# A factorised interaction network: one transfer per shifted tile from a DRAM copy of x, products of 2048 columns in a hand-written order, and weights prepared by another route

## The chip, the core and the metric

The kernel runs on one core of a Trainium2 chip. The metric is the device time of one execution in microseconds. The engines are TensorE (PE, matmuls into PSUM; PEld are its weight loads), VectorE (DVE), ScalarE (ACT), GpSimd (POOL) and SyncE (SP). SP, ACT and POOL can issue transfers (DMA) between DRAM and SBUF, the on-chip memory of 128 partitions.

## What is computed

The input x has 1024 samples of 39 fields of 64 embedding values. Three layers take products of fields:

```python
def _cin_layer(Xk, X0, W, b):
    O = W.shape[0]
    Hk, Fdim = (Xk.shape[1], X0.shape[1])
    Wr = W.reshape(O, Hk, Fdim)
    return jnp.einsum('bhe,bfe,ohf->boe', Xk, X0, Wr) + b[None, :, None]
X0 = sparse_embedding
Xk = X0
outs = []
for W, b in ((W0, b0), (W1, b1), (W2, b2)):
    Xk = _cin_layer(Xk, X0, W, b)
    outs.append(Xk.sum(axis=-1))
cin_output = jnp.concatenate(outs, axis=-1)
return cin_output @ fc_w.T + fc_b
```

Everything is float32. Each layer has 64 outputs; the result is one number per sample.

## The kernel before

**The algebra.** A column is one (sample, embedding) pair: 65536 columns of 39 values. The second and third layer reach the output only through fc_w, so the weights are contracted first, on the chip: V1 and V2 are 64 x 39 tables made from W1, W2 and fc_w, and T (64 x 39 x 39) is W1 contracted with V2. Then y is a sum over columns of X1 (Z + fc0) + c x, where X1 and Z are two 64-row results of one matrix product over the 780 unordered pairs of fields of a column.

**Pairs by shifted tiles.** A tile r_i (i = 0 to 3) has 117 partitions, three groups of 39 rows; each group holds x with its fields rolled by some shift. The elementwise product of two such tiles holds 117 pairs per column. Six products of two tiles and a seventh, of r_0 with a tile q of [x shifted by 17; x; ones], give all pairs, the squares and x itself. So a column costs seven products on VectorE and seven accumulated matmul chunks on PE, whose weights `wt` hold [T | W0] rows gathered to match the pairs.

**Blocks.** The loop over n takes 32 blocks of 2048 columns (`BLK`). SP issues all of a block's transfers, in this order: the load of 39 rows of x into the first group of r_0 (L175, runs of 64 values), two copies of these rows into r_0's other groups (L178, L179), nine copies with a shift into r_1 to r_3 (L183), and two into q (L184, L185). Each is 39 rows of 8 KB, 312 KB, from SBUF to SBUF but for the load. The copies wait for the load, and shifted copies read rows that earlier copies wrote. The r tiles have two buffers each, so a block's transfers can run while the block before is computed.

**The inner loop.** Each block has two halves of 1024 columns (`SUB`). For each half VectorE makes seven products p (L193, ten buffers), and PE takes each in two matmuls of 512 columns into a PSUM tile po (L195; the profile counts a float32 matmul as two instructions, 56 per block). When a half is done, ACT adds the bias to X1 (L204) and copies x's rows into g (L206), VectorE forms (Z + fc0) X1 (L207) and sums over the 64 embedding values (L209). The order on each engine is chosen by the framework's scheduler. At the very end two matmuls with a column of ones and c (L216) and ACT (L217) give y.

**Weights.** ACT issues the loads of w1 and w2, then fc. V2 comes from eight matmuls of one output row (L103), each copied by VectorE (L105) and spread by a transfer of its own (L106); V1 the same way in five (L114 to L117). T comes from five matmuls (L122), copied into `table` beside W0 (L123). The table is written four times, doubled both ways, to DRAM (`wide`, L131), and 39 gathers on ACT (L137) read it into wa and wb by strided rows, so that a roll needs no wrap. `wt` is wa + wb (L148): one addition that waits for all gathers.

**Semaphores.** Transfers issued by SP and ACT signal their landing on eight semaphores (DMAHW0 to DMAHW7 in the rows below), used again and again by both queues; a transfer that takes a semaphore waits until the one before it on that semaphore has landed. POOL's transfers have eight of their own (DMASW).

Of the kernel before, what the change touches and what calls it, by code (L numbers as in the profile page):

```python
# [24 lines left out]
[x shifted by LAST; x; 1], gives that one, the squares and x itself.  # L25
"""
# [16 lines left out]
SHIFT = ((0, 1, 3, 10), (0, 4, 15, 20), (0, 6, 14, 27))  # L43
LAST = 17
# [6 lines left out]
SB = SUB // E  # L51

_dist = sorted(
    min((s[k] - s[i]) % F, (s[i] - s[k]) % F) for s in SHIFT for i, k in PAIRS
)
assert sorted(_dist + [LAST]) == list(range(1, F // 2 + 1))


@with_exitstack
def cin_kernel(ctx: ExitStack, tc: tile.TileContext, x, w0t, b0, w1, b1, w2, b2, fc_w, fc_b, out):  # L60
    nc = tc.nc
    PSUM = bass.MemoryType.PSUM

    const = ctx.enter_context(tc.tile_pool(name="const", bufs=1))
    prep = ctx.enter_context(tc.tile_pool(name="prep", bufs=2))
    dram = ctx.enter_context(tc.tile_pool(name="dram", bufs=1, space=bass.MemoryType.DRAM))
# [3 lines left out]
    ps_prep = ctx.enter_context(tc.tile_pool(name="ps_prep", bufs=2, space=PSUM))  # L70
    ps_main = ctx.enter_context(tc.tile_pool(name="ps_main", bufs=3, space=PSUM))

# [1 line left out]
    w1s = const.tile([H, FH], F32, name="w1s")  # L74
    nc.scalar.dma_start(w1s, w1)
    w2s = const.tile([H, FH], F32, name="w2s")
    nc.scalar.dma_start(w2s, w2)
    fc = const.tile([H, 3], F32, name="fc")
    nc.scalar.dma_start(fc, fc_w.rearrange("o (l h) -> h (o l)", h=H))
# [8 lines left out]
    # table[b, a] = [T[:, a, b] | W0[:, a, b]]  # L88
    table = const.tile([F, F, 2 * H], F32, name="table")
    nc.scalar.dma_start(table[:, :, H:], w0t)  # L90
# [3 lines left out]
    wt = const.tile([K, NCHUNK, 2 * H], F32, name="wt")  # L94
    nc.vector.memset(wa[:, NCHUNK - 1, :], 0.0)
    nc.vector.memset(wb[:, NCHUNK - 1, :], 0.0)

# [1 line left out]
    v2 = const.tile([H, F], F32, name="v2")  # L99
    for g in range(8):  # L100
        n = 8 * F
        pv = ps_prep.tile([128, MM], F32, name="pv", tag="pp")
        nc.tensor.matmul(pv[0:1, :n], fc[:, 2:3], w2s[:, g * n : (g + 1) * n], start=True, stop=True)  # L103
        vrow = prep.tile([1, MM], F32, name="vrow", tag="vrow")
        nc.vector.tensor_copy(vrow[:, :n], pv[0:1, :n])  # L105
        nc.scalar.dma_start(v2[8 * g : 8 * g + 8, :], vrow[:, :n])  # L106

# [1 line left out]
    w1v = w1s.rearrange("o (h f) -> o f h", f=F)  # L109
    for g in range(5):  # L110
        f0, f1 = 8 * g, min(8 * g + 8, F)
        n = (f1 - f0) * H
        pv = ps_prep.tile([128, MM], F32, name="pv", tag="pp")
        nc.tensor.matmul(pv[0:1, :n], fc[:, 1:2], w1v[:, f0:f1, :], start=True, stop=True)  # L114
        vrow = prep.tile([1, MM], F32, name="vrow", tag="vrow")
        nc.vector.tensor_copy(vrow[:, :n], pv[0:1, :n])  # L116
        nc.scalar.dma_start(wa[2 * F + f0 : 2 * F + f1, NCHUNK - 1, 0:H], vrow[:, :n])  # L117
    for g in range(5):
        f0, f1 = 8 * g, min(8 * g + 8, F)
        n = (f1 - f0) * H  # L120
        pt = ps_prep.tile([128, MM], F32, name="pt", tag="pp")
        nc.tensor.matmul(pt[0:F, :n], v2, w1v[:, f0:f1, :], start=True, stop=True)  # L122
        nc.vector.tensor_copy(  # L123
            table[:, f0:f1, 0:H], pt[0:F, :n].rearrange("p (f h) -> p f h", h=H)
        )

# [1 line left out]
    wide = dram.tile([2 * F, 2 * F, 2 * H], F32, name="wide")  # L128
    for i in range(2):
        for k in range(2):  # L130
            nc.scalar.dma_start(wide[i * F : (i + 1) * F, k * F : (k + 1) * F, :], table)  # L131
    pair_rows = wide.rearrange("b a h -> (b a) h")

    def gather(dst, c, j, sa, sb):
        first = sb * 2 * F + sa
        step = 2 * F + 1
        nc.scalar.dma_start(  # L137
            dst[j * F : (j + 1) * F, c, :], pair_rows[first : first + (F - 1) * step + 1 : step, :]
        )

    for c, (i, k) in enumerate(PAIRS):
        for j in range(NG):
            gather(wa, c, j, SHIFT[j][i], SHIFT[j][k])
            gather(wb, c, j, SHIFT[j][k], SHIFT[j][i])
    gather(wa, NCHUNK - 1, 0, 0, LAST)
    gather(wb, NCHUNK - 1, 0, LAST, 0)
    gather(wa, NCHUNK - 1, 1, 0, 0)
    nc.vector.tensor_tensor(wt, wa, wb, ALU.add)  # L148

# [1 line left out]
    wfin = const.tile([H + F, 1], F32, name="wfin")  # L151
    nc.vector.memset(wfin[0:H], 1.0)
    pc = ps_prep.tile([128, MM], F32, name="pc", tag="pp")
    nc.tensor.matmul(pc[0:F, 0:1], v2, bias[:, 0:1], start=True, stop=True)  # L154
# [9 lines left out]
    for i in range(2):  # L164
        qt = const.tile([K, BLK], F32, name=f"q{i}")
        nc.gpsimd.memset(qt, 1.0)  # L166
        q.append(qt)
# [93 lines left out]
```

## Time and profile before

| | |
|---|---|
| median of 3 runs | 1157.2 us (1156.73 to 1162.63) |
| the profiled execution, first to last instruction | 1157.6 us |
| PE busy | 887.4 us, 77% |
| DVE busy | 682.9 us, 59% |
| ACT busy | 140.9 us, 12% |
| POOL busy | 3.7 us |
| mean granted clock of PE | 0.915 |
| moved by DMA | 149.09 MB, mean 129 GB/s |

The profile comes from one execution. Its page gives each engine's busy time; the chain that ended last (followed back from the last instruction, at each step to whatever released it); groups of instructions by line with total and mean duration and what ended the idle time before them; and transfers by queue. Other views list instructions in order of time, or give per stretch of time each engine's busy time, the granted clock, the busy share of the 16 DMA engines and the GB/s moved. In the chain "SPq L183" is time in which SP's queue was busy issuing that line's transfers, and "DMA r<-in_x" is time from an issue to the landing. A transfer landed when the engine waiting for it goes on.

### The profile page before, as it was taken

To read this page: it belongs to the slowest core of one execution; us is meant where nothing else is said; L and a number is where in the kernel's file an instruction comes from. 1 tells how busy PE (TensorE), PEld (TensorE's weight loads), DVE (VectorE), ACT (ScalarE), POOL (GpSimd) and SP (SyncE) were. 2 spreads that over 40 slices of the span, in tenths; PEclk is the share of its full clock that TensorE was granted. 3 is DMA by queue.
4 is the path that set the end of the run, shared out by engine and by line. 5 is a ranking of instruction groups with operands and counts; after the bars stand their busy time and mean duration, and the time that the engine had idled before them with its cause. 6 is when DMAs were issued, how large, how long until landed. Compare 5 with 4: busy or idle time off the path is not lost.

```text
span 1157.6 us, 5508 instructions
## 1 busy us (share of the span) xinstructions
PE 887.4 (77%) x1838; PEld 364.8 (32%) x1838; DVE 682.9 (59%) x598; ACT 140.9 (12%) x133; POOL 3.7 (0%) x6
## 2 busy tenths in 40 slices
PE   2700798988887878898787887987778788788887
PEld 0000343333333333333333333332333333333333
DVE  0330567667766656667655566575556666766555
ACT  1000012111111111101111111011111111111111
POOL 1000000000000000000000000000000000000000
PEclk9999999999888888998888889988988998888889
DMA  8463256556556565556566655555665555656650
GB/s 134 110 141 92 60 135 146 133 130 136 136 131 135 135 149 134 127 131 141 130 138 135 140 129 134 130 136 128 140 148 134 127 136 132 142 132 141 142 138 6
DMA packets 66601, 149.09 MB, mean 129 GB/s; under 512 B 48543, under 2 KB 50064, under 8 KB 50065
## 3 DMA queue, kind: packets, MB, share of 16 engines
q1 hardware_dynamic: 61986, 143.16, 54.6%
q10 hardware_dynamic: 4586, 5.59, 2.4%
q8 instruction: 14, 0.23, 0.1%
q14 instruction: 15, 0.11, 0.0%
HBM read 12.67 MB, written 3.12 MB: 14 GB/s over the span
## 4 chain that ended last, share of the span: by engine, by line
SPq 49%; DMA 37%; PE 9%; ACTq 2%; issue 2%; DVE 1%; ACT 0%; DVEq 0%
SPq L183 41%; DMA r<-in_x 17%; DMA r<-r 14%; PE po L195 7%; SPq L185 4%; SPq L184 3%; ACTq L137 2%; DMA v<-vrow 1%; DMA wide<-table 1%; DMA fc<-in_fc_w 1%; PE pt L122 1%; DMA q<-r 1%; DVE p L193 0%; DMA wa<-wide 0%; DMA wa<-vrow 0%
## 5 line engine op out<-in xcount | busy, mean ns | idle before, releaser
L195 PE MATMUL po<-p,wt 117*128 117x512 f32 x1792 | 855.9, 639 | 231.6 <-DVE p L193 149.9
L195 PEld LDWEIGHTS po<-p,wt 117*128 117x128 f32 x1792 | 360.9, 205 | 726.2 <-issue 418.0
L193 DVE TENSOR_TENSOR p<-r,r 117x1024 f32<-117x1024 f32 x384 | 451.1, 1217 | 135.6 <-DMA r<-r 123.5
L207 DVE SCALAR_TENSOR_TENSOR g<-po,fc,x 64x1024 f32<-64x1024 f32 x64 | 81.6, 1276 | 228.0 <-ACT x L204 228.0
L204 ACT ACTIVATE x<-po,b0s 64x1024 f32<-64x1024 f32 x64 | 71.1, 1110 | 760.4 <-PE po L195 760.4
L206 ACT COPY g<-r 39x1024 f32<-39x1024 f32 x64 | 66.8, 1044 | 199.2 <-DVE sums L209 196.3
L193 DVE TENSOR_TENSOR p<-r,q 117x1024 f32<-117x1024 f32 x64 | 77.8, 1216 | 5.4 <-DMA q<-r 4.6
L209 DVE TENSOR_REDUCE sums<-g 103x16 f32<-103x1024 f32 x64 | 77.6, 1212 | 1.1
L148 DVE TENSOR_TENSOR wt<-wa,wb 117x896 f32<-117x896 f32 x1 | 1.1, 1093 | 54.8 <-DMA wa<-wide 54.8
L103 PE MATMUL pv<-w2s,fc 64*1 64x312 f32 x16 | 8.9, 709 | 23.0 <-DMA fc<-in_fc_w 17.2
L105 DVE COPY vrow<-pv 1x312 f32<-1x312 f32 x8 | 3.6, 468 | 29.8 <-PE pv L103 17.9
L114 PE MATMUL pv<-w1s,fc 64*1 64x512 f32 (+1 forms) x10 | 9.7, 1093 | 4.0 <-DVE vrow L105 2.3
L103 PEld LDWEIGHTS pv<-w2s,fc 64*1 64x1 f32 x16 | 1.2, 94 | 29.6 <-DMA w2s<-in_w 17.2
L122 PE MATMUL pt<-w1s,v 64*39 64x512 f32 (+1 forms) x10 | 9.6, 1104 | 0.8 <-DVE table L123 0.8
L216 PE MATMUL py<-sums,wfin 103*1 103x512 f32 x4 | 3.2, 880 | 7.7 <-DVE sums L209 7.7
L123 DVE COPY table<-pt 39x512 f32<-39x512 f32 (+1 forms) x5 | 3.3, 670 | 7.3 <-PE pt L122 7.3
L116 DVE COPY vrow<-pv 1x512 f32<-1x512 f32 (+1 forms) x5 | 3.2, 662 | 7.1 <-DMA wa<-vrow 3.7
L114 PEld LDWEIGHTS pv<-w1s,fc 64*1 64x1 f32 x10 | 0.6, 87 | 12.4 <-DVE vrow L116 6.5
L122 PEld LDWEIGHTS pt<-w1s,v 64*39 64x39 f32 x10 | 1.4, 157 | 9.0 <-DVE table L123 4.2
L206 ACT ACT_TABLE_LOAD x1 | 1.3, 1283 | 21.8 <-DMA v<-vrow 21.8
L155 ACT COPY wfin<-pc 39x1 f32<-39x1 f32 x1 | 0.2, 151 | 28.0 <-PE pc L154 28.0
L166 POOL MEMSET q<- 117x2048 f32 x2 | 3.5, 1804 | 0.3 <-POOLq L248 0.3
(16 smaller groups left out, 3.7 us busy)
## 6 DMA issues: line engine op xcount, KB each, us to landing
r<-r SPq DMA_DIRECT2D x352, 312.0 KB
q<-r SPq DMA_DIRECT2D x64, 312.0 KB
r<-in_x SPq DMA_DIRECT2D x32, 312.0 KB
wide<-table ACTq DMA_DIRECT2D x4, 760.5 KB
w1s<-in_w ACTq DMA_DIRECT2D x1, 624.0 KB
w2s<-in_w ACTq DMA_DIRECT2D x1, 624.0 KB
wa<-wide ACTq DMA_DIRECT2D x20, 19.5 KB
table<-in_w0t ACTq DMA_DIRECT2D x1, 380.2 KB
```

The costliest lines, as they stand in the source:

```text
L114: nc.tensor.matmul(pv[0:1, :n], fc[:, 1:2], w1v[:, f0:f1, :], start=True, stop=True)
L122: nc.tensor.matmul(pt[0:F, :n], v2, w1v[:, f0:f1, :], start=True, stop=True)
L137: nc.scalar.dma_start(dst[j * F : (j + 1) * F, c, :], pair_rows[first : first + (F - 1) * step + 1 : step, :])
L183: nc.sync.dma_start(r[i][j * F : (j + 1) * F], r[0][s : s + F])
L184: nc.sync.dma_start(qt[0:F], r[0][LAST : LAST + F])
L185: nc.sync.dma_start(qt[F : 2 * F], r[0][0:F])
L193: nc.vector.tensor_tensor(p, a[:, cols], b[:, cols], ALU.mult)
L195: nc.tensor.matmul(po[:, bass.ts(m, MM)], wt[:, c, :], p[:, bass.ts(m, MM)], start=(c == 0), stop=(c == NCHUNK - 1),)
L204: nc.scalar.activation(x1, po[H:128, :], AF.Identity, bias=b0s[H:128])
L206: nc.scalar.copy(g[H : H + F], r[0][0:F, cols])
L207: nc.vector.scalar_tensor_tensor(g[0:H], po[0:H, :], fc[:, 0:1], x1, ALU.add, ALU.mult)
L209: nc.vector.tensor_reduce(sums[:, b_at : b_at + SB], g.rearrange("p (b e) -> p b e", e=E), AX.X, ALU.add)
```

## The change

- **A copy of x in DRAM.** `load(n)` brings a block's 39 rows to a staging tile xs; `store(n)` writes them twice, one under the other, to a tile xd of 78 rows in DRAM; `roll(n)` reads each r_i from there in one transfer of 117 rows of 8 KB (936 KB), with rows of the three groups interleaved: partition 3f + j holds x[f + BASE[i] + j STEP[i]]. The shifts form such steps now (STEP, BASE; LAST is 11). q takes its two sets of rows from xd too. A block has 9 transfers instead of 14.
- **Order by hand.** The framework's scheduler is off (`manual_schedule`); each engine takes its instructions as they are written. SP: roll(n + 1), load(n + 2), store(n + 2). VectorE: a product covers 2048 columns (`BLK`, four buffers); the last block's results (`finish`) stand behind this block's fourth product. PSUM is one pool of four two-bank tiles.
- **x's rows for g** are copied from xs, not from r_0.
- **Weights.** fc is the first transfer on ACT, w2 the first on SP. W0 goes from DRAM to a doubled table in DRAM on POOL (`wide0`), and its 15 gathers are POOL's. V2 comes from eight matmuls of 32 equal output rows each, put under each other in PSUM, two copies and two transfers. V2 doubled, with fc1 as two more columns, is the left operand of the five matmuls for T, so that V1 comes out as a row of the same product; each of the five parts is copied and stored twice to DRAM (`wide`, L194) at once. Gathers of T go out on ACT (into wa, L201) and SP (into wb). Each chunk's wa + wb is its own addition (L284), behind that chunk's product of block 0, and the matmuls take wa.

```diff
+STEP = (0, 15, 9, 6)
+BASE = (0, 3, 5, 20)
+LAST = 11
...
+def rows(t, first, steps, n):
+    base = t[:]
+    width = base.ap[-1][1] if len(base.ap) == 2 else n
+    ap = [[s * width, k] for s, k in steps] + [[1, n]]
+    return bass.AP(base.tensor, base.offset + first * width, ap)
...
-    prods = ctx.enter_context(tc.tile_pool(name="prods", bufs=10))
+    prods = ctx.enter_context(tc.tile_pool(name="prods", bufs=4))
...
+    ctx.enter_context(tc.manual_schedule())
...
+    def load(n):
+        xs[n] = stage.tile([F, BLK], F32, name="xs", tag="xs")
+        nc.sync.dma_start(
+            xs[n].rearrange("p (b e) -> p b e", e=E), xv[:, n * BB : (n + 1) * BB, :]
+        )
+    def store(n):
+        xd[n] = xds.tile([FW, BLK], F32, name="xd", tag="xd")
+        nc.sync.dma_start(xd[n][0:F], xs[n])
+        nc.sync.dma_start(xd[n][F:FW], xs[n])
+    def roll(n):
+        r[n] = [rolls.tile([K, BLK], F32, name=f"r{i}", tag=f"r{i}") for i in range(4)]
+        for i in range(4):
+            nc.sync.dma_start(r[n][i], rows(xd[n], BASE[i], [(1, F), (STEP[i], NG)], BLK))
+        qt = q[n % 2]
+        nc.sync.dma_start(qt[0:K:NG], xd[n][LAST : LAST + F])
+        nc.sync.dma_start(qt[1:K:NG], xd[n][0:F])
...
+    for half in range(2):
+        for t in range(4):
+            g = 4 * half + t
+            nc.tensor.matmul(pv[32 * t : 32 * t + 32, half, 0:n8], fc2,
+                w2s[:, g * n8 : (g + 1) * n8], start=True, stop=True)
+    for half in range(2):
+        nc.vector.tensor_copy(vrow[:, half], pv[:, half, 0:n8])
+        nc.scalar.dma_start(v2[32 * half : 32 * half + 32, 0:F], vrow[0:128:32, half])
+    nc.vector.tensor_copy(v2[:, F:FW], v2[:, 0:F])
...
+        nc.tensor.matmul(pt[0:FX, :n], v2, w1v[:, f0:f1, :], start=True, stop=True)
+        part = const.tile([FX, MM], F32, name=f"part{g}")
+        nc.vector.tensor_copy(part[:, :n], pt[0:FX, :n])
+        for k in range(2):
+            nc.scalar.dma_start(widev[:, (k * F + f0) * H : (k * F + f1) * H], part[:, :n])
...
+    for c, (i, k) in enumerate(PAIRS):
+        gather(nc.scalar, wa[:, c], wide, i, k, tcol)
+        gather(nc.sync, wb[:, c], wide, k, i, tcol)
...
+    store(1)
...
-                p = prods.tile([K, SUB], F32, name="p")
-                nc.vector.tensor_tensor(p, a[:, cols], b[:, cols], ALU.mult)
+        p = prods.tile([K, BLK], F32, name="p", tag="p")
+        nc.vector.tensor_tensor(p, a, b, ALU.mult)
...
+            nc.scalar.copy(gt[H : H + F], xs[n][:, bass.ts(h, SUB)])
...
+    for n in range(NBLK):
+        if n + 1 < NBLK:
+            roll(n + 1)
+        if n + 2 < NBLK:
+            load(n + 2)
+            store(n + 2)
+        for c in range(NCHUNK):
+            p = product(n, c)
+            if n == 0:
+                nc.vector.tensor_tensor(wa[:, c], wa[:, c], wb[:, c], ALU.add)
+            multiply(n, c, p)
+            if n > 0 and c == 3:
+                finish(n - 1)
+        fields(n)
+    finish(NBLK - 1)
```

The order on SP in the steady loop, before: one block but for its load and its second q transfer (r_415 is that block's r_0; r_416 to r_418 are r_1 to r_3; in brackets what an instruction waits for).

```order
L178 DMA r_415<-r_415 39x2048 [waits DMAHW5_49,DMAHW4_49]
L179 DMA r_415<-r_415 39x2048 [waits DMAHW6_49]
L183 DMA r_416<-r_415 39x2048 [waits DMAHW7_49,DMAHW5_49]
L183 DMA r_416<-r_415 39x2048 [waits DMAHW0_49]
L183 DMA r_416<-r_415 39x2048 [waits DMAHW1_49]
L183 DMA r_417<-r_415 39x2048 [waits DMAHW2_49]
L183 DMA r_417<-r_415 39x2048 [waits DMAHW3_49]
L183 DMA r_417<-r_415 39x2048
L183 DMA r_418<-r_415 39x2048
L183 DMA r_418<-r_415 39x2048 [waits DMAHW6_49]
L183 DMA r_418<-r_415 39x2048 [waits DMAHW7_49]
L184 DMA q_234<-r_415 39x2048 [waits DMAHW0_49]
```

And now, one block (r_286 to r_289 are the four shifted tiles, q_79 is q):

```order
L118 DMA r_286<-xd 117x1x2048 [waits DMAHW6_49,DMAHW0_49,DVE_49]
L118 DMA r_287<-xd 117x1x2048 [waits DMAHW7_49,DMAHW1_49]
L118 DMA r_288<-xd 117x1x2048 [waits DMAHW2_49]
L118 DMA r_289<-xd 117x1x2048 [waits DMAHW3_49]
L120 DMA q_79<-xd 39x2048 [waits DMAHW4_49]
L121 DMA q_79<-xd 39x2048
L106 DMA xs<-in_x 39x32x64 [waits Activation_49]
L112 DMA xd<-xs 39x2048 [waits DMAHW6_49]
L113 DMA xd<-xs 39x2048 [waits DMAHW0_49]
```

Fourteen transfers have become nine; the store of the block after next, which waits for its load (row 8 on row 7), stands ahead of the next block's rolls, and the first of these rolls waits for the store's first half.

SP in the preparation, now: the last four transfers of block 0's rolls and q, and the first two gathers of T into wb.

```order
L118 DMA r_110<-xd 117x1x2048 [waits DMAHW1_49]
L118 DMA r_111<-xd 117x1x2048 [waits DMAHW2_49]
L120 DMA q_79<-xd 39x2048 [waits DMAHW3_49,Pool_49]
L121 DMA q_79<-xd 39x2048 [waits DMAHW4_49]
L201 DMA wb<-wide 117x1x64 [waits DMAHW6_49,DMAHW5_49]
L201 DMA wb<-wide 117x1x64 [waits DMAHW6_49]
```

DMAHW1 to DMAHW4 are, at these points, the semaphores of ACT's gathers into wa, so r_110 and r_111 (r_2 and r_3 of block 0) wait for gathers to land, and the gathers into wb stand behind all of them in SP's queue. Six more gathers and the store of block 1 follow.

VectorE in the steady loop, before: twelve instructions from the second product of one half of a block to the results of a half before the next half's fourth product.

```order
L193 TENSOR_TENSOR p<-r_415,r_417 117x1024 [waits DMAHW4_49,DMAHW3_49,DMAHW2_49]
L193 TENSOR_TENSOR p<-r_416,r_417 117x1024
L207 SCALAR_TENSOR_TENSOR g<-po,fc,x_409 64x1024 [waits Activation_49]
L209 TENSOR_REDUCE sums<-g 103x16 [waits DVE_49]
L193 TENSOR_TENSOR p<-r_415,r_418 117x1024 [waits DMAHW7_49,DMAHW6_49,DMAHW5_49]
L193 TENSOR_TENSOR p<-r_416,r_418 117x1024
L193 TENSOR_TENSOR p<-r_417,r_418 117x1024
L193 TENSOR_TENSOR p<-r_415,q_234 117x1024 [waits DMAHW1_49,DMAHW0_49]
L193 TENSOR_TENSOR p<-r_415,r_416 117x1024
L193 TENSOR_TENSOR p<-r_415,r_417 117x1024
L193 TENSOR_TENSOR p<-r_416,r_417 117x1024
L207 SCALAR_TENSOR_TENSOR g<-po,fc,x_462 64x1024 [waits Activation_49]
```

And now, one block:

```order
L237 TENSOR_TENSOR p<-r_286,r_287 117x2048 [waits DMAHW1_49,DMAHW0_49,PE_49]
L237 TENSOR_TENSOR p<-r_286,r_288 117x2048 [waits DMAHW2_49,DVE_49,PE_49]
L237 TENSOR_TENSOR p<-r_287,r_288 117x2048 [waits DVE_49,PE_49]
L237 TENSOR_TENSOR p<-r_286,r_289 117x2048 [waits DMAHW3_49,DVE_49,PE_49]
L267 SCALAR_TENSOR_TENSOR g<-po,fc,x_398 64x1024 [waits Activation_49]
L271 TENSOR_REDUCE sums<-g 103x16 [waits DVE_49]
L267 SCALAR_TENSOR_TENSOR g<-po,fc,x_400 64x1024 [waits Activation_49]
L271 TENSOR_REDUCE sums<-g 103x16 [waits DVE_49]
L237 TENSOR_TENSOR p<-r_287,r_289 117x2048 [waits PE_49]
L237 TENSOR_TENSOR p<-r_288,r_289 117x2048 [waits PE_49]
L237 TENSOR_TENSOR p<-r_286,q_79 117x2048 [waits DMAHW5_49,DMAHW4_49,PE_49]
```

A product is twice as wide, and the two pairs for the block before (L267, L271; L207 and L209 above) stand together behind the fourth product, which waits for PE to give back a buffer.

More of the change, by code (lines that the diff above doesn't have):

```diff
@@ new lines, in roll @@
+    def roll(n):
[5 more added lines that the diff above has]
+        nc.sync.dma_start(qt[1:K:NG], xd[n][0:F])
+    w2s = const.tile([H, FH], F32, name="w2s")
+    nc.sync.dma_start(w2s, w2)
+    fc = const.tile([H, 3], F32, name="fc")
+    nc.scalar.dma_start(fc, fc_w.rearrange("o (l h) -> h (o l)", h=H))
@@ L112, in cin_kernel @@
         n = (f1 - f0) * H
[L113 to L125, printed above, removed]
@@ L145, in cin_kernel @@
[L145 to L154, printed above, removed]
+        pt = psum.tile([128, SUB], F32, name="pt", tag="po")
+        nc.tensor.matmul(pt[0:FX, :n], v2, w1v[:, f0:f1, :], start=True, stop=True)
@@ new lines, in cin_kernel, with product, multiply @@
+    nc.scalar.activation(kfin, pc[0:1, MM : MM + 1], AF.Identity, bias=fcb, scale=float(E))
+    sums = const.tile([H + F, B], F32, name="sums")
+    po, g = {}, {}
+    def product(n, c):
+        a, b = (r[n][PAIRS[c][0]], r[n][PAIRS[c][1]]) if c < len(PAIRS) else (r[n][0], q[n % 2])
+        p = prods.tile([K, BLK], F32, name="p", tag="p")
+        nc.vector.tensor_tensor(p, a, b, ALU.mult)
+        return p
+    def multiply(n, c, p):
+        if c == 0:
+            po[n] = [psum.tile([128, SUB], F32, name="po", tag="po") for _ in range(BLK // SUB)]
+        for m in range(BLK // MM):
+            nc.tensor.matmul(
+                po[n][m // 2][:, bass.ts(m % 2, MM)],
+                wa[:, c, :],
+                p[:, bass.ts(m, MM)],
+                start=(c == 0),
+                stop=(c == NCHUNK - 1),
+            )
```

168 lines of the change are left out of this document (88 added, 80 removed).

## The prediction

> **What bounds the kernel now.** I read the page's chain of waits first, then its groups of instructions, then the issues of SP in order of time. In the chain each figure is a share of the span:
>
> ```profile
> SPq 49%; DMA 37%; PE 9%; ACTq 2%; issue 2%; DVE 1%; ACT 0%; DVEq 0%
> SPq L183 41%; DMA r<-in_x 17%; DMA r<-r 14%; PE po L195 7%; SPq L185 4%; SPq L184 3%; ACTq L137 2%; DMA v<-vrow 1%; DMA wide<-table 1%; DMA fc<-in_fc_w 1%; PE pt L122 1%; DMA q<-r 1%; DVE p L193 0%; DMA wa<-wide 0%; DMA wa<-vrow 0%
> ```
>
> 86% is SP issuing transfers and transfers landing; TensorE has 9%. So the 77% busy PE is not the bound; the queue that feeds it is. One block of 32 in that queue (start, duration):
>
> ```profile
> 530.13 1.34 SPq L175 DMA_DIRECT2D r<-in_x  x1
> 536.76 0.79 SPq L178 DMA_DIRECT2D r<-r  x1
> 537.61 0.75 SPq L179 DMA_DIRECT2D r<-r  x1
> 541.93 17.16 SPq L183 DMA_DIRECT2D r<-r  x9
> 559.14 1.73 SPq L184 DMA_DIRECT2D q<-r  x1
> 560.91 2.26 SPq L185 DMA_DIRECT2D q<-r  x1
> 563.28 1.19 SPq L175 DMA_DIRECT2D r<-in_x  x1
> ```
>
> Load to load is 33.2 us, a serial chain: the load lands after 6.6, the first copy after 5.2, then eleven issues in 21.4. Against it stand, per block, what the engines need:
>
> ```profile
> L195 PE MATMUL po<-p,wt x39: 592/592/593, 503.6 to 519.9; 117*128 117x512 f32 x39
> L193 DVE TENSOR_TENSOR p<-r,r 117x1024 f32<-117x1024 f32 x384 | 451.1, 1217 | 135.6 <-DMA r<-r 123.5
> L207 DVE SCALAR_TENSOR_TENSOR g<-po,fc,x 64x1024 f32<-64x1024 f32 x64 | 81.6, 1276 | 228.0 <-ACT x L204 228.0
> L209 DVE TENSOR_REDUCE sums<-g 103x16 f32<-103x1024 f32 x64 | 77.6, 1212 | 1.1
> L204 ACT ACTIVATE x<-po,b0s 64x1024 f32<-64x1024 f32 x64 | 71.1, 1110 | 760.4 <-PE po L195 760.4
> ```
>
> 39 matmuls in a dense stretch start over 16.3 us, 0.429 us apart; a block has 56 of them, so 24.0 us. VectorE: 14 products, 451.1/384 = 1.175 us of busy time each, 16.4, and 2 x (1.276 + 1.212) = 5.0, in all 21.4 us. ACT is far below. So 33.2 falls to 24.0 at best by this change's main part.
>
> **The blocks after the change.** PE's 56 matmuls, ACT's four instructions and the reductions stay. Seven products of 2048 columns stand for 14 of 1024: at twice 1.175 the same 16.4 us, a little less for seven starts saved; I count 21.4 for VectorE, hidden under PE's 24.0. The products may run four ahead. finish(n-1) stands behind the fourth product, and behind its waiting instruction three products queue on VectorE; the fourth product itself waits for PE to release the last block's last buffer, so x1 is 1.1 us away by then, and PE has three products of 3.4 us in hand against 2.4 + 5.0 us. Without that cover PE would lose up to 5.0 us a block.
>
> What is late next is SP's new chain, which is still serial: six rolls (r0 to r3, two q), the load of the block after, the store that waits for that load, and the next roll that waits for the store. Its period D adds up from these rows (one-microsecond windows: DMA share and GB/s are the last two columns; then two pieces of the chain):
>
> ```profile
> 537.00:538.00 1.00, 1.00 (x4) 0.44 (x3) 1.00 (x2) 0.00 (x0) 0.00 (x0) 1.00 0.00 0
> 538.00:539.00 1.00, 1.00 (x4) 0.51 (x3) 1.00 (x2) 0.00 (x0) 0.00 (x0) 1.00 0.87 213
> 3.00:3.50 0.50, 0.00 (x0) 0.00 (x0) 0.00 (x0) 0.00 (x0) 0.50 (x1) 1.00 2.04 306
> 58.00:68.00 10.00, 0.00 (x0) 0.00 (x0) 8.82 (x8) 0.00 (x0) 0.00 (x0) 1.00 0.79 204
> 133.86 4.70 DMA r<-in_x
> 138.58 5.09 DMA r<-r
> ```
>
> - From issue to first data: the copy issued at 536.76 moves nothing until after 538: 1.4 us.
> - Rolls and q: 3+3+3+3+1+1 = 14 times 312 KB, 4.47 MB, one more than the 13 of before, now all read from DRAM. The trace has no such transfer. Slow end: nine rolls of before in 17.16 us, 168 GB/s, give 26.6 us. Fast end: 306 GB/s, the best half microsecond of loads from DRAM (w1, w2 and x, into 64 and 39 partitions), gives 14.6. I take 14.6: 168 GB/s went into 39 rows out of 39 rows, 306 into 64 rows; the rate grows with the rows reached, and a roll now writes 117 rows at once and reads none of SBUF.
> - Load: alone it landed in 4.70, so behind the rolls it adds 3.3. In the stream of before the two q, about 1.9 us each, drained until 531.9, and it landed at 536.76: 4.9. I take 3.9.
> - Store: its nearest row is the pair of copies, 5.09 to the first's landing; only the first half gates r0, the second r1. It now goes to DRAM; the 58 to 68 window, when 3 MB went to DRAM beside copies at 204 GB/s, gives no sign of a slow writer. I take 5.1; bounds are 4.7, the landing of the tiny `v<-vrow` quoted below, and 6.6, that of the load in the stream.
>
> D = 1.4 + 14.6 + 3.9 + 5.1 = **25.0 us**, just over PE's 24.0. Its bounds are 24.0 and 39.5.
>
> The Trainium skill, "DMA: Bandwidth & Descriptors", section on the anatomy of one DMA, speaks against the store: a completion waits for the write's receipt, which it calls surprisingly long when the target is HBM. It puts the fixed cost near 2 us; that the receipt from HBM is later than the one inside the 5.1 no run here shows, and the third rival below prices it from rows. "SBUF — State Buffer", section on the DMA port swizzle, has a rule for the rate: 39 partitions from 0 reach 8 of the 16 ports, 117 reach all. The trace agrees in direction, 168 against 306 GB/s; by its 27 GB/s per port eight ports are worth 217.
>
> **The start and the end.** The first matmul of the products came at 122.75 us; before it stood these pieces:
>
> ```profile
> 2.01 15.08 DMA fc<-in_fc_w
> 18.96 4.66 DMA v<-vrow
> 48.42 7.54 PE pt L122 x8
> 57.01 16.97 DMA wide<-table
> 116.79 4.63 DMA wa<-wide
> 122.75 9.79 PE po L195 x16
> ...
> 17.23 4.31 PE L103 MATMUL pv<-w2s,fc 64*1 64x312 f32 x8 [17.23 <-DMA fc<-in_fc_w]
> ...
> 2.00:9.00 7.00, 0.00 (x0) 0.00 (x0) 0.00 (x0) 0.00 (x0) 2.27 (x2) 1.00 1.05 165
> ```
>
> V2 goes to its tile in two transfers instead of eight, V1 comes with T out of one product, 39 gathers on ACT become 8 there, 8 on SP and 15 on POOL, and no gather waits for the 17 us of `wide<-table`. In the new order: w1 and w2, 1.28 MB at 165 GB/s, are in at 10 us (at worst 17, as before); 16 matmul passes at 4.31/8 = 0.54 make 8.6, 18.6; copy and one v2 transfer 0.5 + 4.7, 23.8; ten passes of T at 0.94 make 9.4, 33.2; last copy and store 0.7 + 4.6, 38.5; first gathers on ACT another 4.6, 43. Here the program's waits cost something: r2 of block 0 waits for ACT's second gather, r3 and the q's for later ones, and SP's wb gathers queue behind them: 8 of the train's 14 parts, 8.3 us, so **PE starts at about 52** (bounds 42 and 70). PE's first microseconds run at the low clock, as after any pause (granted clock 0.50):
>
> ```profile
> 555.00:559.00 4.00, 1.26 (x2) 0.78 (x3) 2.56 (x3) 1.04 (x1) 0.00 (x0) 0.50 0.69 150
> ```
>
> 16 matmuls took 9.8 instead of 6.9 us: 3 us. At the end, before:
>
> ```profile
> 1124.76 24.30 PE po L195 x52
> 1154.77 0.68 ACT y L217
> ```
>
> From PE's last product at 1149.06 to the end of the span were 8.5 us; finish now does both halves behind it, one more pair of 2.5: 11 us.
>
> **The sum**, against the profiled execution (1157.6 us span; the median of the runs is 1157.2, so no correction). If PE sets the pace: 52 + 3 + 32 x 24.0 + 11 = 834. If SP's chain does: block 2's rolls issue at 52 + 5.1 (store of block 1) + 1.4 + 14.6 + 3.9 + 5.1 = 82; 29 periods later block 31's; r0 and r1 are 6/14 of the train, so 1.4 + 6.3 + 0.6, one product 2.3, PE's 24 and 1 us for r3 coming after it, 11 at the end: 82 + 10.6 + 25 + 11 + 29 x D = 128.6 + 29 D, with D = 25.0 **853 us**. The chain is late by more than PE's lead from block 10 or so.
>
> **Rivals.** (1) PE sets the pace all the way, D under 24.3: 834, and 824 if PE starts at 42. For it: only 1 us separates the two; against it: the chain has three landings in a row, any of which can be late. (2) The reads from DRAM run slower than the best half microsecond: at the 204 GB/s of the mixed window the train takes 21.9, D is 32.3, 1065 us; at 255 GB/s D is 27.9, 938. For it: no long window of before is faster than 204; against it: all of those had the narrow 39-row transfers in them. (3) The store, now to DRAM, lands later: at its bound of 6.6 D is 26.5, 897 us. For it: nothing of before waits for a write to DRAM but `wide<-table`, 17 us for ten times the bytes beside other traffic; against it: that is no slower per byte than the copies. (4) **Slower than before**: the train still goes at the 168 GB/s of L183, because what limits there is neither source nor rows but the way one queue's 8 KB rows are worked off. Then 26.6, D is 37.0, 1202 us. It decides from 128.6 + 29 D = 1157, D = 35.5, 25.1 us for the train, 178 GB/s. For it: the same queue and row size; against it: 213 GB/s in the window quoted, with 39 rows. (5) The change does not do what it says: the rolls are issued as one transfer each, but the eight completion semaphores, shared by SP and ACT, hold one of them back for an earlier landing in every block. One more landing of 5.1 makes D 30.1, 1002 us. For it: nine transfers a block share eight; against it: in the order each waits for one that the chain had to wait for anyway.
>
> **Chances.** Forecast, D of 24.3 to 26, 834 to 883: 0.45. Rival 1: 0.18. Rival 2: 0.18, half of it under 940. Rival 3: 0.09. Rival 4: 0.06. Rival 5: 0.04. The range reaches from 818 to 940 and leaves out some 0.2. Faster by over 0.5% (about what a measurement of this kernel can tell from no change) 0.93, within 0.01, slower 0.06.
>
> **What would show it.** The chain of waits should be DMA and SPq at a period near 25 us, with PE's share up; PE busy near 95% between 60 and 830, granted clock near 1.0; DMA GB/s in the first 15 us after r0's issue near 300; first matmul of L244 near 52. I am wrong if the rolls land later than 17 us after issue, if DVE rather than DMA is what PE waits for, or if PE pauses long enough for clock 0.50 to return.

## The result, and the profile after

The changed kernel takes 896.3 us (median of four runs, 888.91 to 906.01) against 1159.9 (1156.73 to 1163.75) for the kernel before in the same comparison. The ratio is 0.770, with a 95% interval of 0.765 to 0.775. The forecast was 853 with a range of 818 to 940: the direction is right and the range holds the time, which lies 43 us above the forecast. Ratios here leave out slow runs, those over 1.5% above the fastest of the same kernel, while medians take in all of them; the profiled execution, 906.0 us, is such a run, so its rows stand some 10 us above the median.

First the page after, with the span, the busy time of the engines, the chain of waits by engine and by line, and the two costliest groups (busy, mean ns of one, then idle time before them and what ended most of it):

```profile
span 904.2 us, 4982 instructions
PE 808.2 (89%) x1828; PEld 344.5 (38%) x1828; DVE 659.8 (73%) x372; ACT 140.8 (16%) x133; POOL 15.0 (2%) x25
DMA 79%; SPq 14%; PE 2%; DVE 2%; issue 2%; ACT 0%; ACTq 0%; DVEq 0%
DMA xs<-in_x 54%; DMA xd<-xs 20%; SPq L118 8%; SPq L120 3%; SPq L121 2%; DMA r<-xd 2%; DMA v<-vrow 1%; SPq L112 1%; PE pt L190 1%; DMA q<-xd 1%; PE po L244 1%; DVE p L237 1%; DMA fc<-in_fc_w 1%; DMA wide<-part 1%; DVE g L267 1%
L244 PE MATMUL po<-p,wa 117*128 117x512 f32 x1792 | 794.0, 603 | 70.8 <-DVE p L237 47.0
L237 DVE TENSOR_TENSOR p<-r,r 117x2048 f32<-117x2048 f32 x192 | 431.7, 2286 | 195.5 <-DMA r<-xd 173.7
```

The kernel moves more bytes than before (179.36 MB, 149.09 then). PE is busy 89% of the span and yet holds 2% of the chain. What PE waited for is a product of VectorE; what VectorE waited for before its products is r from xd; and the chain goes on to the load (`xs<-in_x`) and the store (`xd<-xs`), 74% together. Before, SP's issues had half of the chain; now the landings have 79%. The load's 54% is not the cost of a load: it starts at the load's issue, when the rolls ahead of it still move their data. That is seen in the issues of SP in order of time (start, duration), two blocks:

```profile
397.02 4.07 SPq L118 DMA_DIRECT2D r<-xd  x4
402.70 0.54 SPq L106 DMA_DIRECT2D xs<-in_x  x1
415.55 0.31 SPq L112 DMA_DIRECT2D xd<-xs  x1
...
420.11 4.10 SPq L118 DMA_DIRECT2D r<-xd  x4
...
425.83 0.54 SPq L106 DMA_DIRECT2D xs<-in_x  x1
443.95 0.31 SPq L112 DMA_DIRECT2D xd<-xs  x1
448.49 0.84 SPq L118 DMA_DIRECT2D r<-xd  x1
```

This is the serial chain that the prediction added up. From the rolls' first issue to the load's landing (the start of L112) the first block takes 18.5 us, the second 23.8; from the store's issue to the next rolls both take 4.5. So the periods are 23.1 and 28.4 us. The mean over the loop comes from the first issue of block 2's rolls and of block 31's:

```profile
83.38 4.11 SPq L118 DMA_DIRECT2D r<-xd  x4
...
853.90 4.03 SPq L118 DMA_DIRECT2D r<-xd  x4
```

(853.90 - 83.38) / 29 = **26.57 us**, where 25.0 was predicted. Why two blocks with the same bytes differ by 5 us shows in the windows of both (busy time of the engines, granted clock, busy share of the DMA engines, GB/s):

```profile
398.00:403.00 5.00, 5.00 (x13) 2.17 (x12) 5.00 (x3) 0.00 (x0) 0.00 (x0) 1.00 0.72 283
403.00:408.00 5.00, 5.00 (x13) 2.28 (x12) 2.67 (x2) 0.00 (x0) 0.00 (x0) 1.00 0.82 339
408.00:413.00 5.00, 5.00 (x13) 2.18 (x12) 4.73 (x3) 2.22 (x2) 0.00 (x0) 1.00 0.84 310
...
421.00:426.00 5.00, 5.00 (x13) 2.28 (x12) 5.00 (x3) 0.00 (x0) 0.00 (x0) 1.00 0.69 251
426.00:431.00 5.00, 5.00 (x13) 2.16 (x12) 0.45 (x1) 0.00 (x0) 0.00 (x0) 1.00 0.81 277
431.00:436.00 5.00, 4.33 (x11) 1.75 (x10) 2.29 (x1) 2.22 (x2) 0.00 (x0) 1.00 0.83 265
436.00:441.00 5.00, 4.46 (x11) 1.82 (x10) 4.37 (x2) 0.00 (x0) 0.00 (x0) 1.00 0.68 153
441.00:444.00 3.00, 3.00 (x8) 1.33 (x7) 3.00 (x3) 0.00 (x0) 0.00 (x0) 1.00 0.09 24
```

Rolls, q and load are 4.47 + 0.32 MB. The first block moves 4.66 MB in 15 us, 311 GB/s; the second needs 20 us for 4.73 MB, 237 GB/s, with the DMA engines about as busy at first: the same packets take longer. And its end drags: in the last 3 us before the load has landed the engines are busy to 0.09, the work of one or two of 16 (0.09 x 16 = 1.4), and the landing waits for them. From 431 to 441 PE gets 11 matmuls in 5 us instead of 13: it has run out of products.

### The profile page after: what moved, and what is told of

It is laid out like the page before. It is cut to its first block, busy times and chain, and to the rows that moved or that the text cites. A ratio compares the mean times of both kernels' runs of the same rounds, so it can differ in the third digit from the quotient of the medians.

```text
span 904.2 us, 4982 instructions
## 1 busy us (share of the span) xinstructions
PE 808.2 (89%) x1828; PEld 344.5 (38%) x1828; DVE 659.8 (73%) x372; ACT 140.8 (16%) x133; POOL 15.0 (2%) x25
## 2 busy tenths in 40 slices
DMA packets 67819, 179.36 MB, mean 198 GB/s; under 512 B 46548, under 2 KB 46747, under 8 KB 47544
## 4 chain that ended last, share of the span: by engine, by line
DMA 79%; SPq 14%; PE 2%; DVE 2%; issue 2%; ACT 0%; ACTq 0%; DVEq 0%
DMA xs<-in_x 54%; DMA xd<-xs 20%; SPq L118 8%; SPq L120 3%; SPq L121 2%; DMA r<-xd 2%; DMA v<-vrow 1%; SPq L112 1%; PE pt L190 1%; DMA q<-xd 1%; PE po L244 1%; DVE p L237 1%; DMA fc<-in_fc_w 1%; DMA wide<-part 1%; DVE g L267 1%
## 5 line engine op out<-in xcount | busy, mean ns | idle before, releaser
L244 PE MATMUL po<-p,wa 117*128 117x512 f32 x1792 | 794.0, 603 | 70.8 <-DVE p L237 47.0
L237 DVE TENSOR_TENSOR p<-r,r 117x2048 f32<-117x2048 f32 x192 | 431.7, 2286 | 195.5 <-DMA r<-xd 173.7
L244 PEld LDWEIGHTS po<-p,wa 117*128 117x128 f32 x1792 | 341.2, 193 | 522.8 <-issue 429.6
L256 ACT COPY g<-xs 39x1024 f32<-39x1024 f32 x64 | 66.7, 1043 | 328.1 <-DVE sums L271 328.1
L267 DVE SCALAR_TENSOR_TENSOR g<-po,fc,x 64x1024 f32<-64x1024 f32 x64 | 81.2, 1269 | 5.7 <-ACT x L263 5.7
L271 DVE TENSOR_REDUCE sums<-g 103x16 f32<-103x1024 f32 x64 | 78.1, 1220 | 2.2
L237 DVE TENSOR_TENSOR p<-r,q 117x2048 f32<-117x2048 f32 x32 | 73.1, 2283 | 0.8 <-issue 0.8
L190 PE MATMUL pt<-w1s,v 64*80 64x512 f32 (+1 forms) x10 | 9.5, 1109 | 11.5 <-DVE v L180 11.5
L284 DVE TENSOR_TENSOR wa<-wa,wb 117x128 f32<-117x128 f32 x7 | 2.0, 285 | 10.0 <-DMA wb<-wide 10.0
L169 PE MATMUL pv<-w2s,fc 64*32 64x312 f32 x16 | 2.3, 724 | 6.9 <-DVE fc L158 6.9
L192 DVE COPY part<-pt 80x512 f32<-80x512 f32 (+1 forms) x5 | 3.4, 674 | 6.8 <-PE pt L190 6.8
L180 DVE COPY v<-v 64x39 f32<-64x39 f32 x1 | 0.2, 176 | 10.4 <-DMA v<-vrow 10.4
L201 POOL DMA_DIRECT2D wb<-wide x6 | 4.5, 744 | 0.0
L201 POOL DMA_DIRECT2D wa<-wide x6 | 4.2, 704 | 11.7 <-DMA wide<-in_w0t 11.6
## 6 DMA issues: line engine op xcount, KB each, us to landing
wide<-in_w0t POOLq DMA_DIRECT2D x4, 380.2 KB, 10.2
```

The source lines that it names most:

```text
L190: nc.tensor.matmul(pt[0:FX, :n], v2, w1v[:, f0:f1, :], start=True, stop=True)
L201: engine.dma_start(dst[:, cols], rows(table, first, steps, H))
L237: nc.vector.tensor_tensor(p, a, b, ALU.mult)
L244: nc.tensor.matmul(po[n][m // 2][:, bass.ts(m % 2, MM)], wa[:, c, :], p[:, bass.ts(m, MM)], start=(c == 0), stop=(c == NCHUNK - 1),)
L256: nc.scalar.copy(gt[H : H + F], xs[n][:, bass.ts(h, SUB)])
L267: nc.vector.scalar_tensor_tensor(gt[0:H], po[n][h][0:H, :], fc[:, 0:1], x1[h], ALU.add, ALU.mult)
```

## The experiments

All were compared with the kernel before, whose median was 1158 to 1160 us in each comparison.

| run | what differs from the changed kernel | median us (lowest to highest) | ratio to the kernel before, 95% interval |
|---|---|---|---|
| x1_floor | no transfers in the loop after block 1 | 837.9 (837.46 to 839.15) | 0.719 to 0.725 |
| x2_threechunks | three of seven chunks on PE | 899.3 (891.42 to 908.07) | 0.764 to 0.773 |
| x3_ahead | loads one block further ahead | 838.9 (838.11 to 839.38) | 0.720 to 0.726 |
| x4_split | three transfers for each r_i | 926.6 (921.11 to 927.67) | 0.794 to 0.801 |
| x5_sbuf | as x4_split, out of SBUF | 1194.2 (1190.47 to 1196.05) | 1.026 to 1.032 |
| x6_contig | load of 39 contiguous rows | 890.0 (883.75 to 895.79) | 0.763 to 0.773 |
| x9_swap | first rolls wait for the whole store | 951.9 (948.68 to 966.51) | 0.817 to 0.822 |
| x8_both | x3_ahead, gathers moved to ACT | 837.2 (835.11 to 837.32) | 0.720 to 0.723 |
| x10_ahead_three | x3_ahead, three chunks on PE | 753.8 (749.25 to 757.41) | 0.644 to 0.653 |
| x11_start | x8_both, block 0's rolls on POOL's queue | 835.3 (834.23 to 836.49) | 0.717 to 0.723 |
| x12_group | rows of a tile group by group | 2050.6 (2048.94 to 2052.93) | 1.761 to 1.775 |

### Is it the chain, or PE?

x1_floor takes the transfers out of the loop:

```diff
-        if n + 1 < NBLK:
+        if n == 0:
             roll(n + 1)
-        if n + 2 < NBLK:
-            load(n + 2)
-            store(n + 2)
+        if n > 0 and n + 1 < NBLK:
+            r[n + 1], xs[n + 1] = r[n - 1], xs[n - 1]
```

> Leaves out all loads, stores and rolls after block 1: the blocks use the shifted tiles of blocks 0 and 1 again, so the sums are those of two blocks. Theory (SP's serial chain of rolls, load, store sets the pace): PE's 24.0 us a block are left, 54 + 3 + 32 x 24.0 + 11 = 836 us. Rival (PE by itself needs more than 24.0 us a block, by waits on VectorE or a lower clock): 870 us or more, hardly under the changed kernel.

837.9 us, as the theory said, and PE has 94% of the chain. x2_threechunks leaves the transfers and takes most of PE's work out:

```diff
-            multiply(n, c, p)
+            if c in (0, 4, NCHUNK - 1):
+                multiply(n, c, p)
```

> Leaves out the matmuls of four of the seven chunks; all products and transfers stay. PE needs 10.3 us a block in place of 24.0. Theory (SP's chain): the period of 26.5 us stays, only the last block's matmuls are shorter, 870 to 890 us. Rival (PE sets the pace): VectorE's 21.4 us a block are left, 54 + 32 x 21.4 + 15 = 755 us.

899.3 us, no change, with PE busy 52% of the time. The page of x2_threechunks (busy times, chain):

```profile
PE 461.9 (52%) x804; PEld 182.9 (21%) x804; DVE 659.3 (74%) x372; ACT 140.8 (16%) x133; POOL 15.0 (2%) x25
DMA xs<-in_x 53%; DMA xd<-xs 20%; SPq L118 8%; SPq L120 3%; SPq L121 3%; DMA r<-xd 2%; DMA q<-xd 1%; SPq L112 1%; PE pt L190 1%; DMA v<-vrow 1%; DVE p L237 1%; PE po L244 1%; DMA fc<-in_fc_w 1%; DMA wide<-part 1%; DVE g L267 1%
```

The chain is the same to a percent. So PE does not set the pace of the changed kernel, and its reads of SBUF are not seen to slow the transfers either: they went down to three sevenths and the time stayed. The expected gain of x2_threechunks (870 to 890) did not come.

### Are the bytes too many, or the waits?

x3_ahead moves the same bytes, but the store of block n + 2 finds its load landed a block ago, and the load behind it is waited for by nobody in this block:

```diff
-    stage = ctx.enter_context(tc.tile_pool(name="stage", bufs=3))
+    stage = ctx.enter_context(tc.tile_pool(name="stage", bufs=4))
...
     store(1)
+    load(2)
...
         if n + 2 < NBLK:
-            load(n + 2)
             store(n + 2)
+        if n + 3 < NBLK:
+            load(n + 3)
```

> The same transfers, but the load is issued one block earlier (four staging buffers), so that the store doesn't wait for a load that stands behind the rolls. Theory (the serial chain, by its waits for landings): the period falls to PE's 24.0 or little over, 836 to 850 us. Rival (the traffic itself, whatever its order): period near 26, 880 us or more.

838.9 us, the time of x1_floor: all of the chain's cost is gone though no byte is. SP's rows and what PE waited for in x3_ahead (in the last row: us in total, times, longest):

```profile
409.17 3.46 SPq L118 DMA_DIRECT2D r<-xd  x4
...
414.24 0.54 SPq L112 DMA_DIRECT2D xd<-xs  x1
...
415.29 0.34 SPq L106 DMA_DIRECT2D xs<-in_x  x1
432.20 3.43 SPq L118 DMA_DIRECT2D r<-xd  x4
```

```profile
PE po L245 <- DVE wa L286: 23.8, 1, 23.8
```

The store (L112) now follows the q transfers at once, where in the two blocks of the changed kernel it stood 13 and 18 us behind the load's issue. The row shown is PE's one wait in the blocks, for block 0's weights; no wait for a product is left. x10_ahead_three takes four of PE's seven chunks out of x3_ahead:

> The load one block earlier, and the matmuls of four of the seven chunks left out, so that PE (10.3 us a block) no longer covers what the transfers cost without the waits. Theory (it was the waits for landings that cost, not the traffic): VectorE's 21.4 us a block are the next bound, 54 + 32 x 21.4 + 15 = 755 us, up to 790. Rival (the traffic of 17 times 312 KB a block is itself worth 24 us or more): 840 us or more, no faster than with all matmuls.

753.8 us. Without the load's landing in its way the loop runs at 21.3 us a block (SP issues block 2's rolls at 88.17 and block 31's at 706.51), with VectorE busy 87%. x2_threechunks made the same cut and gained nothing; the difference between the two is the load's landing in the chain. The theory's 755 us came, but not by its mechanism alone. The chain of x10_ahead_three, by engine:

```profile
DMA 68%; SPq 16%; DVE 10%; issue 3%; PE 3%; ACT 0%; ACTq 0%; DVEq 0%
```

Transfers, not VectorE, hold most of it (53% is the store's landing, which now stands behind the rolls). So at 21.3 us a block the traffic of one block and VectorE's 21.4 us of work lie close together, and the match with 755 is in part luck. What is shown is that the traffic fits into less than PE's 24.0 us.

### What the form of the transfers is worth

x4_split reads each r_i in three transfers of 39 rows; x5_sbuf does the same out of the staging tile, which is doubled by one copy, and makes no copy in DRAM:

```diff
-            nc.sync.dma_start(r[n][i], rows(xd[n], BASE[i], [(1, F), (STEP[i], NG)], BLK))
+            for j in range(NG):
+                first = BASE[i] + j * STEP[i]
+                nc.sync.dma_start(r[n][i][j:K:NG], xd[n][first : first + F])
```

```diff
+        xd[n] = xs[n]
+        nc.sync.dma_start(xs[n][F:FW], xs[n][0:F])
-        xd[n] = xds.tile([FW, BLK], F32, name="xd", tag="xd")
-        nc.sync.dma_start(xd[n][0:F], xs[n])
-        nc.sync.dma_start(xd[n][F:FW], xs[n])
```

> Each shifted tile is read from DRAM in three transfers of 39 rows in place of one of 117; same bytes, same rows. Theory (the source in DRAM and the rows written make the rate, not the form of one transfer): period up by at most 1.5 us for more issues and waits, 890 to 940 us. Rival (the one wide transfer makes it): 14 transfers at 1.9 us each as in the kernel before, period near 35, 1100 us.

> As the run with three transfers a tile, but the rows come from the staging tile in SBUF, doubled there by one copy, in place of DRAM. Theory (the source made the rate: 39 rows of SBUF give 168 to 217 GB/s): train 21 to 27 us, period 30 to 35, 1000 to 1150 us. Rival (it is the order and the rows written, the source does not matter): 927 us as with the source in DRAM.

926.6 us, inside the theory's range, and 1194.2, above the 1150 of its theory. One transfer instead of three is worth 30 us. The source is worth 268 us: from SBUF the same twelve transfers are slow. SP's rows in x4_split, then in x5_sbuf:

```profile
416.61 9.35 SPq L120 DMA_DIRECT2D r<-xd  x12
444.04 9.68 SPq L120 DMA_DIRECT2D r<-xd  x12
```

```profile
459.98 23.20 SPq L119 DMA_DIRECT2D r<-xs  x12
495.74 23.92 SPq L119 DMA_DIRECT2D r<-xs  x12
```

23.20 / 12 = 1.93 us for a copy of 312 KB, as the nine of L183 before (17.16 / 9 = 1.91). The period is 27.4 us in x4_split and 35.8 in x5_sbuf. So the gain of the change hangs on the copy in DRAM, not on the number of transfers, though it takes two writes to DRAM where x5_sbuf makes one copy. Why SBUF is the slower source no run shows.

x12_group keeps one transfer a tile and all the bytes, but orders the 117 rows group by group, as in the kernel before, instead of field by field; q's rows and the weights follow:

```diff
-            nc.sync.dma_start(r[n][i], rows(xd[n], BASE[i], [(1, F), (STEP[i], NG)], BLK))
+            nc.sync.dma_start(r[n][i], rows(xd[n], BASE[i], [(STEP[i], NG), (1, F)], BLK))
```

> The changed kernel with the rows of a shifted tile group by group (partition 39j + f) in place of interleaved (3f + j): the same one transfer of 117 rows per tile, the same bytes, but its rows on the DRAM side now come as 3 sets of 39 in place of 39 sets of 3. The weights are gathered to match. Theory (the form counts only by its bytes and rows): 890 to 910 us as before. Rival (the outermost count sets how many DMA engines share a transfer; the Trainium skill, DMA: Bandwidth & Descriptors, on how many engines, would give 3 engines in place of 13, an estimate): the train takes some four times as long, period 70 us or more, over 2000 us.

2050.6 us, the rival. SP's row for one block's rolls, and a window in them, of x12_group (its last two columns as above, DMA share and GB/s):

```profile
844.19 15.57 SPq L118 DMA_DIRECT2D r<-xd  x4
```

```profile
846.00:856.00 10.00, 10.00 (x20) 4.29 (x20) 4.14 (x2) 0.00 (x0) 0.00 (x0) 0.83 0.19 74
```

The DMA engines are busy to 0.19 and move 74 GB/s, where the changed kernel's train has 0.81 to 0.84 of them at 265 to 339 GB/s. The Trainium skill, "DMA: Bandwidth & Descriptors", has the rule for this in the section on why a DMA increments its semaphore by 16: a transfer is spread over the largest number of engines, at most 16, that divides the outermost size of both sides. A roll's source has 39 as its outermost size in the changed kernel and 3 in x12_group, and both write 117 rows; so the rule gives an estimate of 13 of 16 engines, 0.81, and of 3, 0.19. Both shares of the trace agree. The interleaved row order of the change, which looks like a matter of taste, is a condition of its gain.

### Where the slow blocks come from

Two tries. x6_contig replaces the load's runs of 64 values by 39 contiguous rows of 8 KB (other values of x):

```diff
-            xs[n].rearrange("p (b e) -> p b e", e=E), xv[:, n * BB : (n + 1) * BB, :]
+            xs[n], xc[n * F : (n + 1) * F, :]
```

> The load reads 39 contiguous rows of 8 KB in place of runs of 256 bytes; the values are x in another order, so the sums are those of other pairs. Theory (the load only adds its own 2 to 3 us behind the train): period down by about 1 us, 860 to 880 us. Rival (the small runs disturb the train too, and make its slow blocks): period down to PE's 24, 838 to 850 us.

890.0 us, 6 less than the changed kernel and inside the spread of both: neither expectation came. Some 40,000 packets under 512 B have gone from the page (46548 before, 6612 now) at hardly any gain, and blocks of 27 us remain (rolls issued at 416.21 and 443.51; in x2_threechunks, too, at 415.54 and 442.69). x9_swap stores the halves in the other order, so that r_0 waits for both and no store runs beside the rolls:

```diff
-        nc.sync.dma_start(xd[n][0:F], xs[n])
         nc.sync.dma_start(xd[n][F:FW], xs[n])
+        nc.sync.dma_start(xd[n][0:F], xs[n])
```

> The two halves of the store are issued in the other order, so that r0, which needs the lower half alone, waits for both. That puts r0 about 1.2 us later. Theory (the train is slow in some blocks because its first transfer starts while the store's second half still runs on some of the DMA engines, so that they work out of step and meet at the same rows): train down from 19.5 to about 17, total 870 to 885 us. Rival (the slow blocks have another cause): the delay alone, 29 x 1.2 more, 920 to 930 us.

951.9 us, slower than both expected, and slow blocks remain. SP's rows of x9_swap:

```profile
452.18 0.54 SPq L106 DMA_DIRECT2D xs<-in_x  x1
472.14 0.31 SPq L112 DMA_DIRECT2D xd<-xs  x1
478.27 3.42 SPq L118 DMA_DIRECT2D r<-xd  x4
```

The load landed 20 us after its issue even so, and the store now costs 6.1 us of the chain instead of 4.5. The period, from block 2's rolls to block 31's, is (901.26 - 87.86) / 29 = 28.05 us, 1.5 more than in the changed kernel: nearly all of it is the later store, and the train gained nothing. So the store beside the rolls is not the cause. With x2_threechunks, x6_contig and x9_swap three candidates fall away as the cause (PE's reads, of which x2_threechunks left three sevenths, the load's small packets, the store's second half); what makes the packets of some blocks slower is not settled.

### What the start is worth

x8_both adds to x3_ahead that the gathers into wb go out on ACT instead of behind block 0's rolls on SP; x11_start also issues block 0's rolls on POOL's queue:

```diff
-        gather(nc.sync, wb[:, c], wide, k, i, tcol)
+        gather(nc.scalar, wb[:, c], wide, k, i, tcol)
...
-    roll(0)
+    roll(0, nc.gpsimd)
+    store(1)
+    load(2)
```

> The load one block earlier, and the gathers of T into wb on ACT's queue, each behind its partner, in place of SP's, where they stand behind the rolls of block 0. Theory (those gathers held PE's start): PE starts near 42 in place of 54 us, 827 us. Rival (block 1's rolls are then late, or wb was not what was late): 835 to 839 us.

> The run with the load ahead and all gathers of T on ACT, and in addition block 0's rolls on POOL's queue, ahead of the gathers of W0, and the store of block 1 and the load of block 2 ahead of them on SP, so that no roll of blocks 0 and 1 waits for a gather by a shared semaphore. Theory (PE started at 43 there but then waited for those rolls): the first three blocks run without a pause, 824 to 830 us. Rival (the start is bound by the traffic of two blocks' rolls beside the weights): 835 us or more, no gain.

837.2 and 835.3 us: 2 and 4 less than x3_ahead, with intervals that overlap. In both the rival came. PE's rows and two waits of SP before 70 us (us in total, times, longest) of x8_both, then PE's row of x11_start:

```profile
43.20 6.03 PE L245 MATMUL po<-p,wa 117*128 117x512 f32 x8 [13.20 <-DVE wa L286]
53.10 23.37 PE L245 MATMUL po<-p,wa 117*128 117x512 f32 x48 [3.86 <-DVE wa L286]
78.41 15.70 PE L245 MATMUL po<-p,wa 117*128 117x512 f32 x32 [1.94 <-DVE p L238]
```

```profile
SPq L118 <- DMA wide<-part: 9.4, 2, 9.2
SPq L118 <- DMA wa<-wide: 7.8, 1, 7.8
```

```profile
53.27 67.16 PE L245 MATMUL po<-p,wa 117*128 117x512 f32 x149 [22.07 <-DVE wa L286]
```

In x8_both PE starts 11 us earlier, but it has done only the eight matmuls of one product when it stands until 53.10: the next product waited for a tile of block 0. Block 0's rolls on SP had waited 17 us for stores of T and for a gather, transfers of ACT with which they share semaphores. At 78.41 PE has stood again, for block 1's tiles. In x11_start the rolls are on another queue, but ACT's own queue is the chain: in its issues in order of time the ten stores of T stand from 24.24 for 18.13 us, and the first gather goes out at 48.38, so PE starts at 53.3. That these stores take so long while block 0's rolls move fits the rival, the traffic; no run separates it from other causes. The 11 us did not come in either. Of the versions that compute the whole result x11_start has the lowest median, and it and x3_ahead both beat the changed kernel (896.3) and the one before.

## Why the prediction was right, and where its size was off

**The bound and its new form: right.** SP's chain stays serial: rolls, load, store that waits for the load, next rolls that wait for the store. x3_ahead breaks just that wait and the time falls to PE's 838.9; x1_floor and x2_threechunks say the same from both sides. VectorE's work was hidden as said. One of the prediction's signs of being wrong came by the letter, since in the loop PE waits for VectorE's products (47.0 us) and never for a transfer. But 173.7 of VectorE's own 195.5 us of waiting are for r, so the sign does not speak against the bound.

**The period: 26.57 instead of 25.0, from errors of both signs.** The store takes 4.55 where 5.1 was taken. From the rolls' issue to the load's landing were 1.4 + 14.6 + 3.9 = 19.9 predicted and 26.57 - 4.55 = 22.0 measured. In the fast block quoted it is 18.5, at 311 GB/s, close to the predicted rate of 306: so first data and load cost some 18.5 - 14.6 = 3.9 there, not 5.3. The mean is 3.5 above that block, which puts the mean train near 18.1 us, 247 GB/s (an estimate, if first data and load cost the same in all blocks; the late engines of the slow blocks are in it). **The mis-sized term is the train's 14.6 us**: the best half microsecond of before has the rate of the best blocks, not of the mean. That window's DMA share was a warning: at 2.04 of what 16 engines can be busy, more was put down to it than moved in it. The prediction's own sign for it, rolls that land later than 17 us after issue, was there in the slow blocks (of the 4.47 MB of the second block quoted some 4.0 had moved by 436.0, 16 us after the issue).

The prediction's reason for the rate, that it grows with the rows reached, was wrong too. Each transfer of x4_split and of x5_sbuf writes 39 rows; out of DRAM they cost 30 us in all against the changed kernel, out of SBUF 1.93 us each as before. The source made the 168 GB/s. Nor does the trace show the agreement that the prediction saw with the Trainium skill, "SBUF — State Buffer", section on the DMA port swizzle: by that section 64 partitions from 0 reach the same eight ports as 39, and the 306 GB/s had gone into 64 and 39 of them.

The net is 26.57 - 25.0 = 1.57 us; 29 times this is 46 us, and 853 + 46 = 899. The span of the same execution is 904.2; the other 5 us are the start (block 2's rolls at 83.4, 82 predicted) and the end (50.3 us from block 31's rolls on, 10.6 + 25 + 11 = 46.6 predicted). The median of the runs, 896.3, lies 13 us above the 834 to 883 that the forecast's own periods (24.3 to 26) gave; only the wider range holds it.

**The start: 54.2 against 52, by offsetting errors.** The pieces of the chain up to the first gather of T, then the gathers into wb on SP, and PE's first matmuls of the products (start, duration):

```profile
0.74 5.93 DMA fc<-in_fc_w
6.92 2.35 PE pv L169 x16
10.58 9.86 DMA v<-vrow
20.77 9.51 PE pt L190 x10
31.30 5.35 DMA wide<-part
37.75 4.07 DMA wa<-wide
...
45.19 7.08 SPq L201 DMA_DIRECT2D wb<-wide  x6
...
54.16 21.20 PE L244 MATMUL po<-p,wa 117*128 117x512 f32 x44 [23.52 <-DMA wb<-wide]
```

fc and w2 were in when PE began at 6.9, where 10 was predicted for the weights, and the sixteen passes took 2.35 instead of 8.6 us; v2's transfers took 9.9 instead of 4.7, for a reason that no run shows. T (9.5 against 9.4), its store, the gathers and the 9.0 us from the first gather into wb, behind the rolls, to PE's start (8.3 predicted) came out near their terms. x8_both, where the gathers into wb no longer stand behind the rolls and PE starts at 43.2, shows that they were what PE waited for. PE's slow first microseconds came as well: 5 matmuls from 54 to 58 us and 10 in the next 4, though the granted clock of both windows is 1.00. The prediction puts the low clock after any pause; in the loop PE waited 38 times for a product, up to 3.7 us, and the mean granted clock was 0.985. At the end:

```profile
893.82 1.11 ACT L263 ACTIVATE x<-po,b0s 64x1024 f32<-64x1024 f32 x1 [10.07 <-PE po L244]
```

From there to the end of the span are 10.4 us; 11 were predicted.

**The rivals.** (1) PE sets the pace: not here, but 834 was the right price: x3_ahead, which makes it true, takes 838.9. (2) DRAM reads slower than the best half microsecond: this is what happened, at 247 GB/s by the estimate above; its 938 at 255 came out too high since first data, load and store were cheaper than counted. (3) The store lands later: its 897 is the measured time, by accident. Its mechanism is refuted, since the store took 4.55 and not 6.6. Here the Trainium skill, "DMA: Bandwidth & Descriptors", section on the anatomy of one DMA (written for the path of POOL's transfers; the store is SP's), had spoken against the store, with a receipt that can be late when the target is HBM; by the 4.55 against 5.09 of the copies inside SBUF, no such delay shows. (4) Slower than before: 168 GB/s is the price of SBUF as the source, not of the queue or its 8 KB rows, as this rival had it. x5_sbuf, with that source, comes near the period (35.8 against 37.0) and the time (1194 against 1202) of this rival. (5) Semaphores hold a roll back: not in the loop; but at the start they did, in x8_both and in the changed kernel itself, where block 0's rolls waited 10.2 us for a store of T and 5.4 for a gather.

## What to carry to other kernels

Where a queue's transfers form a loop through their own landings, one more staging buffer that moves a load a block ahead can take the whole loop off the critical path: here a few lines were worth 57 us and reached the time of the kernel without transfers in its loop. To replicate rows over many partitions, a copy in DRAM can beat copies inside SBUF (927 against 1194 us for the same twelve transfers), but the outermost size of the access pattern has to spread it over the engines (896 against 2051). A rate taken from the best half microsecond of a trace is an upper end, and the range should treat it so.

## What the runs showed that was not expected

- The same 4.8 MB took 15 us in some blocks and 20 in others, and slow blocks stayed in x2_threechunks, x6_contig and x9_swap; no run gave the cause.
- The sixteen passes for V2, into four groups of 32 rows of PSUM, took 2.3 us together, 0.15 for each, where one took 0.54 before (4.31 / 8). The group's row has 724 ns for one, five times its share, so several were under way at once:

```profile
L169 PE MATMUL pv<-w2s,fc 64*32 64x312 f32 x16 | 2.3, 724 | 6.9 <-DVE fc L158 6.9
```

- The mean granted clock, 0.985 in the changed kernel, was 0.758 in x2_threechunks and 0.790 in x10_ahead_three, where PE is busy only 52% and 57% of the span. Matmuls of x2_threechunks had a mean of 745 ns instead of 603, which cost nothing, as PE was not the bound.
- One transfer can be worse than three: x12_group with its single transfers took over twice the time of x4_split.
